# An RGCN kernel on one core: products and other uses of PSUM get three fixed banks each instead of six in one ring

## The chip, the core and the metric

The kernel runs on one core of a Trainium2 chip. The metric is the device time of one execution in microseconds (us). Of the engines, PE multiplies matrices and turns tiles (its weight loads are listed apart, as PEld), DVE works on whole tiles, ACT copies and applies functions, POOL issues the gathers, and SP issues the other transfers.

## The reference

Two layers of a relational graph convolution on 50000 nodes of 128 features, then a sum with the input and a layer norm. There are 850000 edges, sorted by their destination, each of one of 16 relations. A relation's matrix is a mixture of 8 basis matrices. Only rows below show the computation.

```python
def _rgcn_layer(h, src, dst, rel, basis, w_comp, loop_w, bias):
    W = jnp.einsum('rb,bio->rio', w_comp, basis)
    seg = dst * N_REL + rel
    agg = jax.ops.segment_sum(h[src], seg, num_segments=N_ENT * N_REL)
    agg = agg.reshape(N_ENT, N_REL, -1)
    msg = jnp.einsum('nri,rio->no', agg, W)
    return jax.nn.relu(msg + h @ loop_w + bias)

h = _rgcn_layer(x, ..., basis1, w_comp1, loop_w1, bias1)
h = _rgcn_layer(h, ..., basis2, w_comp2, loop_w2, bias2)
return _layernorm(x + h)
```

## The kernel before

The edges lie in 6250 tiles of at most 128 slots, and ten tiles (K) make a chunk, so a layer (number n, 0 or 1) has C = 625 chunks. For each tile i, POOL gathers the 128 source rows (`gather`, L254) into one of 40 places (four chunks of ten). PE multiplies them by a matrix of one-hot weights, `hot`, with 8 bases times 12 neighbouring nodes as columns: this is the tile's product (L1018), 128 x 96 in fp32, and it sums the messages by basis and node. DVE adds the product to a ring of node sums in SBUF (`add`, L950), at an offset that is read from memory. The matrix `hot` of a chunk is built on DVE (`hot_of`, L923 and L930) from the weights `pm`.

Every 512 nodes form a group, 98 in a layer, one to about 64 tiles. A group's ring columns are begun with the nodes' own loops (`lay` on ACT, L770, and `own` on DVE, L775, twice a group), copied out once all their edges are added (L792), multiplied by the basis matrices (`base`, L798) and the loop's matrix (L803), passed through relu (L810), turned back (`back`, L822) and stored (in layer 0 by ACT, L830, in layer 1 by DVE with the norm). In layer 0 alone each group's input rows are also turned (`turn`, L726, read by ACT in `turned`, L729), its loop weights combined (`combine`, L743, read by ACT, L754), and every 40 tiles the edges' weights are made (`multiply`, L668, two banks, read by ACT in `kept`, L682).

**Order.** PE, DVE, ACT and POOL run in the order in which the code emits. A loop over chunks and tiles emits the products; a tile's add is emitted twelve products later (BEHIND). All other steps are events in a heap, due at a tile's number (`planned`, `later`), and `go_on` emits what is due after each tile. A read of a bank that has been written by PE is due 12 or 18 tiles after the write.

**Banks.** PSUM has eight banks of 128 x 512 fp32. One is `fixed` (one-hot masks), one is `pn` (bases and loop). The other six are shared by all the rest through `banks`, an object of the class `Turns`. Five consecutive products (PER) share a bank, taken at the first. The taker hands over the read that is to follow (for products: all adds up to the bank's last), and the pool's rotation picks the place:

```python
def take(self, read=None):
    if len(self.held) == self.count:
        first = self.held.pop(0)
        if first is not None:
            first()
    self.held.append(read)
    return self.pool.tile([P, BANK], F32, name=self.name)
```

So a bank comes back after six takes, whoever took it, and if the read of its old content has not been emitted by then, it is emitted at once. The write then waits for that read on its engine.

Of the kernel before, what the change touches and what calls it, by code (L numbers as in the profile page):

```python
# [40 lines left out]
F32 = mybir.dt.float32  # L41
# [7 lines left out]
PSUM = bass.MemoryType.PSUM  # L49
DRAM = bass.MemoryType.DRAM  # L50

P = 128
# [3 lines left out]
K = P // WN  # L56
# [9 lines left out]
PER = 5  # L66
Q = AT // 2
BANK = 512
# [8 lines left out]
BEHIND = 12  # L77
AFTER = 18
AT_ONCE = 4
WIDE = 1  # L80
PARTS_OF = ((0, 3), (3, 5))
EPS = 1e-5
# [7 lines left out]
def tile_rgcn_resnorm(  # L90
# [20 lines left out]
    C = -(-M // (K * P))  # L111
# [106 lines left out]
                    left = less  # L218
            nc.vector.tensor_copy(split[:, n], mine)

    ps_a = ctx.enter_context(tc.tile_pool(name="ps_a", bufs=6, space=PSUM))
    ps_f = ctx.enter_context(tc.tile_pool(name="ps_f", bufs=1, space=PSUM))
    fixed = ps_f.tile([P, BANK], F32, name="fixed")
    ps_n = ctx.enter_context(tc.tile_pool(name="ps_n", bufs=1, space=PSUM))
# [2 lines left out]
    nc.vector.tensor_copy(grid, col[:, :WN])  # L227

    class Turns:
        def __init__(self, pool, name, count):  # L230
            self.pool, self.name, self.count, self.held = pool, name, count, []

        def take(self, read=None):

            if len(self.held) == self.count:
                first = self.held.pop(0)
                if first is not None:
                    first()
            self.held.append(read)
            return self.pool.tile([P, BANK], F32, name=self.name)  # L240

    class Once:
        def __init__(self, what, *args):
# [4 lines left out]
            if what is not None:  # L248
                what(*self.args)

    banks = Turns(ps_a, "pa", 6)

    def gather(to, of, idx):
        return nc.gpsimd.indirect_dma_start(  # L254
# [2 lines left out]

    def turned(h, m, sb):

        tp = ps_a.tile([P, BANK], F32, name="pa")  # L260
        nc.tensor.transpose(tp[:, :m], h, ident[:m, :m])
        hT = sb.tile([P, P], F32, name="hT")
        nc.scalar.copy(hT[:, :m], tp[:, :m])
        return hT[:, :m]
# [342 lines left out]
    def chunked():  # L607
        with (
# [20 lines left out]
            class Weights:  # L629
# [31 lines left out]

                def multiply(self):
                    m = self.m
                    self.po = [banks.take(self.keep) for _ in PARTS_OF]
                    for po, (j0, j1) in zip(self.po, PARTS_OF):
                        of = po[:, : 2 * AT * (j1 - j0) * NB].rearrange("e (n t w) -> e n t w", n=2, t=AT)
                        for j in range(j0, j1):
                            nc.tensor.matmul(  # L668
                                of[:, :, :, (j - j0) * NB : (j - j0 + 1) * NB],
                                self.is_rel[:m, j * P : (j + 1) * P],  # L670
                                each[:m],
                                start=True,
                                stop=True,
                            )
# [17 lines left out]
            class Group:  # L692
# [28 lines left out]

                def turn(self):
                    m = self.m
                    self.po = banks.take(self.keep)
                    for j in range(J):
                        nc.tensor.transpose(self.po[:, j * P : j * P + m], self.h[:m, j, :], ident[:m, :m])  # L726

# [11 lines left out]
                    )  # L739

                def combine(self):
                    self.comb = banks.take(self.combined)
                    nc.tensor.matmul(  # L743
                        self.comb[: 2 * NB, : self.cnt],
                        split[:LOOPS].rearrange("r n b -> r (n b)"),
                        self.is_rel[:LOOPS, : self.cnt],
                        start=True,
                        stop=True,
                    )
# [16 lines left out]
                    )  # L766

                def lay(self, b):
                    self.laid[b] = banks.take(self.owns[b])
                    nc.scalar.copy(self.laid[b][:, : self.cnt], self.hT[:, : self.cnt])  # L770

                def own(self, b):
# [43 lines left out]

                def back(self):
                    m = self.m
                    self.po = banks.take(self.kept)
                    by_place = self.oT[:, : self.cnt].rearrange("o (p j) -> o j p", j=J)  # L820
                    for j in range(J):
                        nc.tensor.transpose(self.po[:m, j * D : (j + 1) * D], by_place[:, j, :], ident)  # L822
# [94 lines left out]
            for n, of in enumerate((x, H1)):  # L917

                def hot_of(c):
# [15 lines left out]
                    )  # L935
                    hots[c] = hot

                def add(c, k, pa):

                    i = c * K + k  # L940
                    if i % (2 * K) == 0:
                        left = min(2, C - c) * K
                        offs = batches[c // BATCH].offs
                        nc.vector.load(at_reg[:left], offs[0:1, c % BATCH * K : c % BATCH * K + left])  # L944
                    if k == 0:
                        for one in groups:
                            assert not first(one.g) <= c <= final(one.g) or one.made
                    at = nc.vector.snap(at_reg[i % (2 * K)], min_val=0, max_val=RING - 1)
                    into = ring[:, :, ds(at, WN)]
                    nc.vector.tensor_tensor(  # L950
                        into,
                        pa[:, k % PER * NB * WN : (k % PER + 1) * NB * WN].rearrange("d (b w) -> d b w", w=WN),
                        into,
                        op=OP.add,
                    )
# [41 lines left out]
                for c in range(C):  # L997
                    if n == 0 and c:

                        next(coming, None)  # L1000
                        while ready[0] + 1 < len(ROWS) and 2 * min(C, c + FETCH + 6) > ROWS[ready[0] + 1]:
                            next(coming)
                    for to in range(0 if c == 0 else c + FETCH, min(C, c + FETCH + 1)):
                        buffer = (n * C + to) % GATHERS
                        for k in range(ks(to)):
                            gather(rows[buffer][:, k, :], of, src[:, to * K + k : to * K + k + 1])
                    g = rows[(n * C + c) % GATHERS]
                    if c == 0:
                        hot_of(0)
                        hot_of(1)  # L1010
                        if n == 0:
                            done(first_runs)
                    hot = hots.pop(c)
                    for k in range(K):
                        if k % PER == 0:
                            pa = banks.take(Once(added_up_to, c * K + k + PER - 1))
                        if k < ks(c):
                            nc.tensor.matmul(  # L1018
                                pa[:, k % PER * NB * WN : (k % PER + 1) * NB * WN],
                                g[:, k, :],  # L1020
                                hot[:, k].rearrange("e b w -> e (b w)"),
                                start=True,
                                stop=True,
                            )
                            behind.append((c * K + k + BEHIND, (c, k, pa)))
                        added_up_to(c * K + k - BEHIND)
                        if c or k == K - 1:
                            go_on(c * K + k)
                    if n == 0 and c == 3:
                        beginning.close()  # L1030
                    if n == 0 and c == C - 1:
                        done(coming)
                        count_up(pr)
                now = C * K
                while events or behind:
                    added_up_to(now - BEHIND)
                    go_on(now)
                    now += 1
                banks.held = [None] * len(banks.held)
            ordered.close()  # L1040

    def summed():
        L1 = dram.tile([N, D], F32, name="L1")
        L2 = dram.tile([N, D], F32, name="L2")
        with tc.tile_pool(name="io", bufs=2) as io, tc.tile_pool(name="sbf", bufs=2) as sb:
# [73 lines left out]
            def added(h, n, L):  # L1119


                def block(r0, p):
# [13 lines left out]
                    for e in range(ROW):  # L1136
# [3 lines left out]
                        msg = sb.tile([P, D], F32, name="msg")  # L1140
                        for b in range(NB):
                            if b % (BANK // D) == 0:
                                mb = ps_a.tile([P, BANK], F32, name="pa")
                                nc.tensor.matmul(
                                    mb[:p, :BANK],
                                    gT,
                                    BASIS[:, b : b + BANK // D, :].rearrange("p b d -> p (b d)"),
                                    start=True,
                                    stop=True,
                                )  # L1150
                            of = mb[:p, b % (BANK // D) * D : (b % (BANK // D) + 1) * D]
                            by = comp[:, e, b : b + 1]
                            if b == 0:
                                nc.vector.tensor_scalar(msg[:p], of, by, None, op0=OP.mult)
                            else:
                                nc.vector.scalar_tensor_tensor(msg[:p], of, by, msg[:p], op0=OP.mult, op1=OP.add)

                        at = tf[:p, e : e + 1]
                        tp = ps_a.tile([P, BANK], F32, name="pa")
                        nc.tensor.transpose(tp[:p, :p], at.to_broadcast([p, p]), ident[:p, :p])  # L1160
                        same = sb.tile([P, P], F32, name="same")
                        nc.vector.tensor_scalar(same[:p, :p], tp[:p, :p], at, None, op0=OP.is_equal)
# [80 lines left out]
```

## Time and profile before

| | |
|---|---|
| median of three runs | 18209.43 us (18202.78 to 18209.78) |
| the profiled execution | 18065.77 us |
| its span | 18063.9 us |
| mean granted clock of PE | 0.602 |
| busy: PE, weight loads | 8315.7 us (46%), 6301.1 us (35%) |
| busy: DVE, ACT, POOL | 6563.7 us (36%), 1621.0 us (9%), 11861.6 us (66%) |
| transfers | 1527.32 MB, 85 GB/s |

A line of the profile's groups names the line of code, the engine, the operation, what is written and read, and the count, then the busy time, the mean in ns, and the idle time of the engine just before, with what ended most of it. "issue" is idle time that ended with nothing the profile shows, "remote" one whose releaser it doesn't know. A line of the waits has the total, the count and the longest. A row of the timeline has the start, the time and in brackets the idle time before it. The starts of matmuls are recorded; their ends are modelled.

### The profile page before, as it was taken

Reading aid. Unit: us, or ns where it says so; the run is one execution under the profiler, and the core shown is the slowest. Engines: PE = TensorE matmul, PEld = TensorE weight load, DVE = VectorE, ACT = ScalarE, POOL = GpSimd, SP = SyncE. Lnnn points to the kernel's source line nnn. Section 1 sums busy time; section 2 is a strip of 40 time slices with the busy share of each in tenths; the row PEclk is TensorE's granted clock in tenths of the full one; section 3 lists DMA queues with packets and bytes.
Section 4 is the critical chain, followed back from the end, with each engine's and each line's share of the span. In section 5 each row is a group of like instructions: output and inputs, shape, how many; then the busy total and the mean of one; then the engine's idle time right before and its main releaser. Section 6 shows DMA issues by size and latency. Waiting matters only on the chain.

```text
span 18063.9 us, 132710 instructions
## 1 busy us (share of the span) xinstructions
PE 8315.7 (46%) x31484; PEld 6301.1 (35%) x31484; DVE 6563.7 (36%) x18253; ACT 1621.0 (9%) x2256; POOL 11861.6 (66%) x12540
## 2 busy tenths in 40 slices
PE   3444444444444444444444444444444444444444
PEld 2333333333333333333333333333333333333333
DVE  5444444443333333333333333333333333333333
ACT  0110011110100000010000000000000000000000
POOL 6666666666666666666666666666666666666665
PEclk7666666666666666666655555555555555555556
DMA  3333333333323322232322222222222222222222
GB/s 100 94 95 92 92 95 95 94 88 89 85 84 85 85 85 82 85 88 83 84 78 81 81 82 79 81 81 81 81 80 80 81 81 81 81 81 81 81 81 67
DMA packets 793018, 1527.32 MB, mean 85 GB/s; under 512 B 229924, under 2 KB 296342, under 8 KB 792230
## 3 DMA queue, kind: packets, MB, share of 16 engines
q0 software_dynamic: 403552, 826.82, 18.0%
q1 hardware_dynamic: 386934, 691.33, 11.6%
q8 instruction: 259, 4.24, 0.1%
q14 instruction: 529, 4.33, 0.1%
q10 hardware_dynamic: 1744, 0.60, 0.0%
HBM read 1390.97 MB, written 126.86 MB: 84 GB/s over the span
## 4 chain that ended last, share of the span: by engine, by line
issue 37%; PE 28%; another core or an unknown queue 16%; POOL 8%; DVE 5%; DMA 3%; ACT 1%; DVEq 1%; POOLq 0%; ACTq 0%; SPq 0%
PE pa L1018 18%; POOL g L254 8%; PE pn L798 8%; DVE ring L950 2%; DMA g<-H,src 2%; DVE ring L775 1%; PE pa L668 1%; PE pn L803 1%; DMA g<-in_x_dram,src 1%; ACT own L792 0%; PE pa L822 0%; DVE fixed L330 0%; DVEq L944 0%; DVE word L333 0%
## 5 line engine op out<-in xcount | busy, mean ns | idle before, releaser
L1018 PE MATMUL pa<-hot,g 128*128 128x96 f32 x25000 | 5704.8, 361 | 7613.1 <-issue 5607.3
L1018 PEld LDWEIGHTS pa<-hot,g 128*128 128x128 f32 x25000 | 5201.3, 276 | 9323.7 <-issue 7321.4
L254 POOL DMA_INDIRECT g<-in_x_dram,src x6250 | 5929.4, 949 | 3046.5 <-issue 1432.7
L254 POOL DMA_INDIRECT g<-H,src x6250 | 5895.2, 943 | 3045.9 <-issue 1428.8
L950 DVE TENSOR_TENSOR ring<-pa,ring 128x96 f32 x12500 | 3212.4, 257 | 10941.4 <-PE pa L1018 5215.2
L798 PE MATMUL pn<-own,basis 128*128 128x512 f32 x3104 | 2237.5, 799 | 508.1 <-issue 486.0
L930 DVE TENSOR_TENSOR hot<-pm,fixed 128x960 f32<-128x960 f32 x1250 | 1443.0, 1154 | 78.9 <-remote 19.2
L792 ACT COPY own<-ring 128x4096 f32<-128x4096 f32 x194 | 699.6, 3606 | 3172.0 <-DVE ring L950 2131.9
L775 DVE TENSOR_TENSOR ring<-wide,pa 128x2048 f32<-128x2048 f32 x392 | 893.7, 2280 | 84.1 <-issue 28.8
L798 PEld LDWEIGHTS pn<-own,basis 128*128 128x128 f32 x3104 | 656.1, 250 | 701.3 <-issue 696.3
L770 ACT COPY pa<-hT 128x512 f32<-128x512 f32 x392 | 230.8, 589 | 3035.4 <-DVE ring L950 1349.5
L726 PE MATMUL pa<-ident,rows 128*128 128x128 f32 x392 | 107.7, 420 | 829.6 <-ACT t L830 452.2
L810 ACT ACTIVATE oT<-pn,bias_of 128x512 f32<-128x512 f32 x196 | 134.3, 685 | 3928.0 <-PE pa L1018 2237.0
L668 PE MATMUL pa<-each,is_rel 128*128 128x128 f32 x1570 | 348.4, 377 | 291.8 <-issue 151.4
L668 PEld LDWEIGHTS pa<-each,is_rel 128*128 128x128 f32 x1570 | 300.5, 276 | 324.0 <-issue 226.2
L726 PEld LDWEIGHTS pa<-ident,rows 128*128 128x128 f32 x392 | 74.6, 223 | 845.1 <-ACT t L830 457.0
L923 DVE TENSOR_TENSOR fixed<-fixed,key 128x120 f32<-128x120 f32 x1250 | 350.4, 280 | 0.1
L822 PE MATMUL pa<-ident,oT 128*128 128x128 f32 (+1 forms) x784 | 218.6, 406 | 201.4 <-issue 133.9
L803 PE MATMUL pn<-hT,loop 128*128 128x512 f32 x392 | 263.1, 740 | 50.1 <-issue 49.9
L682 ACT COPY pm<-pa 128x192 f32<-128x192 f32 x628 | 141.0, 304 | 1063.8 <-remote 903.3
L822 PEld LDWEIGHTS pa<-ident,oT 128*128 128x128 f32 (+1 forms) x784 | 146.7, 219 | 230.2 <-issue 206.0
L597 ACT ACTIVATE sd<-mv,eps 128x4 f32<-128x4 f32 x98 | 29.1, 297 | 1929.9 <-DVE st L594 969.3
(129 smaller groups left out, 1655.8 us busy)
## 6 DMA issues: line engine op xcount, KB each, us to landing
wide<-CW SPq DMA_DIRECT2D x388, 1024.0 KB
g<-in_x_dram,src POOLq DMA_INDIRECT x6250
g<-H,src POOLq DMA_INDIRECT x6250
rows<-in_x_dram SPq DMA_DIRECT2D x194, 256.0 KB
PM<-pm SPq DMA_DIRECT2D x157, 160.0 KB
pm<-PM SPq DMA_DIRECT2D x157, 160.0 KB
H1T<-oT SPq DMA_DIRECT2D x97, 256.0 KB
H<-t SPq DMA_DIRECT2D x97, 256.0 KB
```

Of the source, the lines that this page charges most:

```text
L254: return nc.gpsimd.indirect_dma_start(out=to, out_offset=None, in_=of, in_offset=bass.IndirectOffsetOnAxis(ap=idx, axis=0))
L668: nc.tensor.matmul(of[:, :, :, (j - j0) * NB : (j - j0 + 1) * NB], self.is_rel[:m, j * P : (j + 1) * P], each[:m], start=True, stop=True,)
L770: nc.scalar.copy(self.laid[b][:, : self.cnt], self.hT[:, : self.cnt])
L775: nc.vector.tensor_tensor(ring[:, b : b + AT_ONCE, self.at : self.at + cnt], self.wide.pop(b)[:, :, :cnt], self.laid.pop(b)[:, None, :cnt] ...
L792: nc.scalar.copy(self.sums, ring[:, :, at : at + cnt])
L798: nc.tensor.matmul(self.pn[:, : self.cnt], BASIS[:, b, :], self.sums[:, b, :], start=b == 0, stop=False)
L803: nc.tensor.matmul(self.pn[:, : self.cnt], LOOP, self.hT[:, : self.cnt], start=False, stop=True)
L822: nc.tensor.transpose(self.po[:m, j * D : (j + 1) * D], by_place[:, j, :], ident)
L923: nc.vector.tensor_tensor(own[:, : ks(c)], grid[:, None, :].to_broadcast([P, ks(c), WN]), key[:, c * K : c * K + ks(c), None].to_broadcast ...
L930: nc.vector.tensor_tensor(hot[:, : ks(c)], pm[:, c % BATCH * K : c % BATCH * K + ks(c), :, None].to_broadcast([P, ks(c), NB, WN]), own[:, ...
L950: nc.vector.tensor_tensor(into, pa[:, k % PER * NB * WN : (k % PER + 1) * NB * WN].rearrange("d (b w) -> d b w", w=WN), into, op=OP.add,)
L1018: nc.tensor.matmul(pa[:, k % PER * NB * WN : (k % PER + 1) * NB * WN], g[:, k, :], hot[:, k].rearrange("e b w -> e (b w)"), start=True, st ...
```

## The change

The six places become fixed tiles, `pa0` to `pa5`. A take says among which of them it takes turns: products among the first three (`range(part[0])` with 3 in the table SECTIONS), all other uses of the two layers among the last three (OTHERS). A place that is taken again has its pending read emitted first, as before. Set-up and the unused second path take any of the six. The table's two flags (another order of a bank's products) are off, so products keep their order; the code around them is written for both.

```diff
+SECTIONS = (
+    ((3, False, False),),
+    ((3, False, False),),
+)
+OTHERS = ((3, 4, 5), (3, 4, 5))
...
-    ps_a = ctx.enter_context(tc.tile_pool(name="ps_a", bufs=6, space=PSUM))
+    ps_a = ctx.enter_context(tc.tile_pool(name="ps_a", bufs=1, space=PSUM))
...
     class Turns:
...
+        def __init__(self, tiles):
+            self.tiles, self.held, self.turn = tiles, [None] * len(tiles), {}
+
+        def take(self, read=None, among=None):
+
+            among = tuple(among or range(len(self.tiles)))
+            at = among[self.turn.get(among, 0) % len(among)]
+            self.turn[among] = self.turn.get(among, 0) + 1
+            if self.held[at] is not None:
+                self.held[at]()
+            self.held[at] = read
+            return self.tiles[at]
...
-    banks = Turns(ps_a, "pa", 6)
+    banks = Turns([ps_a.tile([P, BANK], F32, name=f"pa{i}") for i in range(6)])
...
-                    self.po = [banks.take(self.keep) for _ in PARTS_OF]
+                    self.po = [banks.take(self.keep, OTHERS[0]) for _ in PARTS_OF]
...
-                    self.po = banks.take(self.keep)
+                    self.po = banks.take(self.keep, OTHERS[self.n])
...
-                    self.comb = banks.take(self.combined)
+                    self.comb = banks.take(self.combined, OTHERS[0])
...
-                    self.laid[b] = banks.take(self.owns[b])
+                    self.laid[b] = banks.take(self.owns[b], OTHERS[self.n])
...
-                    self.po = banks.take(self.kept)
+                    self.po = banks.take(self.kept, OTHERS[self.n])
...
-                    for k in range(K):
-                        if k % PER == 0:
-                            pa = banks.take(Once(added_up_to, c * K + k + PER - 1))
+                    for at in range(K):
+                        part = SECTIONS[n][c * len(SECTIONS[n]) // C]
+                        k = at // PER * PER + (PER - 1 - at % PER if part[1] and c + 1 < C else at % PER)
+                        if at % PER == 0:
+                            pa = banks.take(
+                                Once(added_up_to, c * K + at + PER - 1), range(part[0])
+                            )
```

The lines of the new file lie 6 to 13 further down: the product is L1031, the add L959, the gather L260, the weights' multiplication L674, the turning L732, the combining L749, the base L804 and the turning back L828.

The first place is on PE in layer 0, about a quarter of the way into PE's list, where a group's weights are combined and the next weights are made. A name has the buffer's number behind it; "waits" names the engines or transfers whose semaphore the instruction waits for. Before:

```order
L743 LDWEIGHTS split_81 [waits DVE_49]
L743 MATMUL pa_22662<-is_lrel_22576,split_81 16x512 [waits Activation_49]
L1018 MATMUL pa_22649<-hot_22506,g3_96 128x96 [waits DMASW1_49]
L798 MATMUL pn_22609<-own_22492,basis_76 128x512
L1018 MATMUL pa_22649<-hot_22506,g3_96 128x96 [waits DMASW2_49]
L1018 MATMUL pa_22649<-hot_22506,g3_96 128x96 [waits DMASW3_49]
L798 MATMUL pn_22609<-own_22492,basis_76 128x512
L1018 MATMUL pa_22689<-hot_22600,g0_93 128x96 [waits DMASW4_49,DVE_49]
L668 MATMUL pa_22697<-each_80,is_rel_22580 128x16x8 [waits Activation_49]
L668 MATMUL pa_22697<-each_80,is_rel_22580 128x16x8 x2
L668 MATMUL pa_22698<-each_80,is_rel_22580 128x16x8 [waits DVE_49,PE_49]
```

The same place after:

```order
L749 LDWEIGHTS split_81
L749 MATMUL pa3_96<-is_lrel_21566,split_81 16x512
L1031 MATMUL pa2_95<-hot_21486,g3_102 128x96 [waits DMASW1_49]
L804 MATMUL pn_21583<-own_21458,basis_76 128x512
L1031 MATMUL pa2_95<-hot_21486,g3_102 128x96 [waits DMASW2_49]
L1031 MATMUL pa2_95<-hot_21486,g3_102 128x96 [waits DMASW3_49]
L804 MATMUL pn_21583<-own_21458,basis_76 128x512
L1031 MATMUL pa0_93<-hot_21574,g0_99 128x96 [waits DMASW4_49,DVE_49]
L674 MATMUL pa4_97<-each_80,is_rel_21570 128x16x8 x3
L674 MATMUL pa5_98<-each_80,is_rel_21570 128x16x8 [waits Activation_49]
```

The instructions stand in the same order. The combining no longer waits at this place, the second of the weights' banks waits for ACT where it waited for DVE and PE, and the product's new bank waits for DVE in both.

The second place is on PE in layer 1, where a group's result is turned back into a bank (`back`), between two products. Before:

```order
L1018 MATMUL pa_65248<-hot_65127,g3_96 128x96 [waits DMASW7_49,DVE_49,PE_49]
L822 MATMUL pa_65256<-ident_72,oT_65137 128x128 [waits DVE_49,PE_49,Activation_49]
L822 MATMUL pa_65256<-ident_72,oT_65137 128x128 x3
L1018 MATMUL pa_65248<-hot_65127,g3_96 128x96 [waits DMASW0_49]
L1018 MATMUL pa_65248<-hot_65127,g3_96 128x96 [waits DMASW1_49]
L1018 MATMUL pa_65248<-hot_65127,g3_96 128x96 [waits DMASW2_49]
L1018 MATMUL pa_65248<-hot_65127,g3_96 128x96 [waits DMASW3_49]
L1018 MATMUL pa_65287<-hot_65196,g0_93 128x96 [waits DMASW4_49,DVE_49,Activation_49]
```

After:

```order
L1031 MATMUL pa0_93<-hot_62268,g3_102 128x96 [waits DMASW7_49,DVE_49]
L828 MATMUL pa5_98<-ident_72,oT_62275 128x128 [waits Activation_49]
L828 MATMUL pa5_98<-ident_72,oT_62275 128x128 x3
L1031 MATMUL pa0_93<-hot_62268,g3_102 128x96 [waits DMASW0_49]
L1031 MATMUL pa0_93<-hot_62268,g3_102 128x96 [waits DMASW1_49]
L1031 MATMUL pa0_93<-hot_62268,g3_102 128x96 [waits DMASW2_49]
L1031 MATMUL pa0_93<-hot_62268,g3_102 128x96 [waits DMASW3_49]
L1031 MATMUL pa1_94<-hot_62334,g0_99 128x96 [waits DMASW4_49,DVE_49]
```

Here, too, nothing moved. The bank `pa0` follows on `pa2` and is followed by `pa1`, so a product's bank was last a product's, and the opening product waits for DVE alone, for the last add of the bank three banks ago, eleven products back.

More of the change, by code (lines that the diff above doesn't have):

```diff
@@ L229, in tile_rgcn_resnorm @@
     class Turns:
[L230 to L240, printed above, removed]
+        def __init__(self, tiles):
[8 more added lines that the diff above has]
+            return self.tiles[at]
     class Once:
@@ L258, in turned @@
     def turned(h, m, sb):
-        tp = ps_a.tile([P, BANK], F32, name="pa")
+        tp = banks.take()
         nc.tensor.transpose(tp[:, :m], h, ident[:m, :m])
@@ L936, in hot_of @@
                     hots[c] = hot
+                pair = [None]
                 def add(c, k, pa):
                     i = c * K + k
-                    if i % (2 * K) == 0:
+                    if (n, i // (2 * K)) != pair[0]:
+                        pair[0] = n, i // (2 * K)
                         left = min(2, C - c) * K
@@ L1024, in chunked @@
                             )
[L1025 to L1028, printed above, removed]
+                            if part[2] and c + 1 < C:
+                                behind.insert(len(behind) - at % PER, (c * K + at // PER * PER + PER - 1 + BEHIND, (c, k, pa)))
+                            else:
+                                behind.append((c * K + at + BEHIND, (c, k, pa)))
+                        added_up_to(c * K + at - BEHIND)
+                        if c or at == K - 1:
+                            go_on(c * K + at)
                     if n == 0 and c == 3:
@@ L1039, in chunked @@
                 banks.held = [None] * len(banks.held)
+                banks.turn.clear()
             ordered.close()
@@ L1142, in block @@
                             if b % (BANK // D) == 0:
-                                mb = ps_a.tile([P, BANK], F32, name="pa")
+                                mb = banks.take()
                                 nc.tensor.matmul(
@@ L1158, in block @@
                         at = tf[:p, e : e + 1]
-                        tp = ps_a.tile([P, BANK], F32, name="pa")
+                        tp = banks.take()
                         nc.tensor.transpose(tp[:p, :p], at.to_broadcast([p, p]), ident[:p, :p])
```

## The prediction

> **What bounds the kernel now.** I read the page's busy line and its groups first, then the list of waits, then two windows of the timeline, and last the table of windows for the two layers apart. The busy line and the four groups that each of the 12500 products passes through:
>
> ```profile
> PE 8315.7 (46%) x31484; PEld 6301.1 (35%) x31484; DVE 6563.7 (36%) x18253; ACT 1621.0 (9%) x2256; POOL 11861.6 (66%) x12540
> ...
> L1018 PE MATMUL pa<-hot,g 128*128 128x96 f32 x25000 | 5704.8, 361 | 7613.1 <-issue 5607.3
> L1018 PEld LDWEIGHTS pa<-hot,g 128*128 128x128 f32 x25000 | 5201.3, 276 | 9323.7 <-issue 7321.4
> ...
> L254 POOL DMA_INDIRECT g<-H,src x6250 | 5895.2, 943 | 3045.9 <-issue 1428.8
> L950 DVE TENSOR_TENSOR ring<-pa,ring 128x96 f32 x12500 | 3212.4, 257 | 10941.4 <-PE pa L1018 5215.2
> ```
>
> No engine is full. POOL, the fullest, waits too, and the list of waits says for whom; so does DVE's largest entry. The columns are the total, the number of waits and the longest:
>
> ```profile
> DVE ring L950 <- PE pa L1018: 5215.2, 1059, 22.6
> DVE ring L950 <- remote: 4149.8, 567, 28.9
> POOL g L254 <- remote: 1603.5, 1256, 8.9
> POOL g L254 <- PE pa L1018: 1295.0, 1639, 8.3
> ```
>
> The gather (L254) waits for a free one of its 40 tiles of rows, which a finished product frees, and the add (L950) waits for the bank's last product. Both wait for the end of products. The price without that wait is in POOL's own beat:
>
> ```profile
> 14008.18 0.94 POOL L254 DMA_INDIRECT g<-H,src  x1 [0.30 <-issue]
> 14009.42 0.94 POOL L254 DMA_INDIRECT g<-H,src  x1 [0.30 <-issue]
> ```
>
> That is 1.24 us a gather, 6250 x 1.24 = 7.75 ms a layer. What a product takes in fact comes from the table of windows, for the product line alone (busy us and records of PE, then of PEld, then the granted clock), the first row in layer 0, the second in layer 1:
>
> ```profile
> 500.00:8500.00 8000.00, 2327.39 (x11082) 2155.47 (x11083) 0.62 0.31 89
> 9500.00:17500.00 8000.00, 2754.29 (x11232) 2480.69 (x11231) 0.58 0.29 81
> ```
>
> A product is two matmul records, so a product takes 8000 / 5541 = 1.444 us in layer 0 and 8000 / 5616 = 1.425 us in layer 1: 9024 and 8903 us for 6250 products. PE's finishing of products sets the pace, 0.2 us a product above POOL.
>
> How far PE is ahead of what it has finished shows in one stretch of layer 0, first PE's weight loads, then DVE, then ACT:
>
> ```profile
> 5050.39 4.77 PEld L1018 LDWEIGHTS pa<-hot,g 128*128 128x128 f32 x22 [1.01 <-ACT pm L682]
> 5054.99 0.71 PEld L822 LDWEIGHTS pa<-ident,oT 128*128 128x128 f32 x4
> 5055.61 0.76 PEld L1018 LDWEIGHTS pa<-hot,g 128*128 128x128 f32 x6
> 5085.96 0.71 PEld L726 LDWEIGHTS pa<-ident,rows 128*128 128x128 f32 x4 [29.59 <-ACT t L830]
> ...
> 5062.94 1.79 DVE L950 TENSOR_TENSOR ring<-pa,ring 128x96 f32 x6
> 5075.52 0.26 DVE L950 TENSOR_TENSOR ring<-pa,ring 128x96 f32 x1 [10.78 <-remote]
> 5076.20 0.82 DVE L950 TENSOR_TENSOR ring<-pa,ring 128x96 f32 x3
> 5087.48 1.43 DVE L950 TENSOR_TENSOR ring<-pa,ring 128x96 f32 x5 [8.90 <-PE pa L1018]
> ...
> 5085.32 0.58 ACT L830 COPY t<-pa 128x512 f32<-128x512 f32 x1 [27.50 <-remote]
> ```
>
> PE starts nothing for 29.59 us, since the turning of the next group's rows (L726) needs a bank that ACT has not read (L830). Yet adds go on until the end of it: products already handed to PE keep coming out. So an idle stretch of PE in this trace is not lost time as such; it counts only where what PE holds runs out.
>
> **The change part by part.** The instructions on PE, DVE, ACT and POOL stay the same in number and shape, so every term is a wait.
>
> *What goes.* In layer 0 a group of 64 products takes 12.8 banks for products and 8.2 for other uses (turn, combine, two layings, back, and two for weights every 40 products). With six banks in one ring a product's bank was often last held by ACT, and the other way round. Products and others now never share a bank, and these waits go, four rows of PE's list:
>
> ```profile
> PEld pa L1018 <- ACT pm L682: 558.7, 58, 38.3
> PEld pa L726 <- ACT t L830: 457.0, 20, 33.2
> PEld pa L1018 <- ACT lrel L754: 315.2, 24, 31.9
> PEld pa L1018 <- ACT hT L729: 116.1, 13, 21.0
> ```
>
> They add up to 1447 us in 115 waits, the most that could be won. The other bound is nothing, as adds go on through them. I take the value from the two layers: layer 1 has no L668, L682, L726, L729, L743 or L754, and its products are 0.0193 us shorter, x 6250 = 120 us. If every one of these blocks cost something, all of that difference is theirs. I take **-120 us**; what hides the rest is the work that PE holds at a block's start, and it would be up to the 1447 us if that cover were not there.
>
> *What comes.* In layer 1 a group takes 12.8 banks for products and three for others. A bank came back after six takes, five or six of them products' as a rule, so that a new bank waited for add i-26 or i-21. With three banks it waits for add i-11, every time, in both layers. When DVE has added everything up to a bank's end, PE holds at most the next ten products; while DVE waits for a bank's last product, PE holds at most that bank and ten more. Behind the waiting product on PE's list stand the other products, and the base matmuls, turns and backs of the groups, for which ACT waits; POOL waits for product j-40, further back still. On DVE one thing moves: the two adds before a new take are emitted ahead of the building of one-hot weights and the layings' products, which wait for those two adds now; DVE was idle for 10941 us before adds, so I put it at nothing, and at its duration of 2 x 0.257 us per chunk, 320 us a layer, if that cover failed.
>
> What ten products are worth as cover: in series 10 x 2 x (361 + 276) ns = 12.7 us, with hidden weight loads 10 x 2 x 361 ns = 7.2 us. DVE's waits for PE of more than 10 us are the places where that runs out, 138 in layer 0 and 181 in layer 1 (sums 1875 and 2480 us). The first and last of each:
>
> ```profile
> 291.01 0.26 DVE L950 TENSOR_TENSOR ring<-pa,ring 128x96 f32 x1 [13.38 <-PE pa L1018]
> 9060.27 0.55 DVE L950 TENSOR_TENSOR ring<-pa,ring 128x96 f32 x2 [19.16 <-PE pa L1018]
> 9165.97 1.43 DVE L950 TENSOR_TENSOR ring<-pa,ring 128x96 f32 x5 [25.29 <-remote]
> 17992.48 1.14 DVE L950 TENSOR_TENSOR ring<-pa,ring 128x96 f32 x4 [15.89 <-PE pa L1018]
> ```
>
> Lower bound: nothing, if PE has enough left each time. Upper bound: at each of them PE stands still for what is over 10 us (670 us in layer 1, 1875 - 1380 = 495 in layer 0) and for the five adds that then free the bank (1.43 us, the row at 9165.97): 670 + 259 + 495 + 197 = 1621 us. I take five adds for each long wait of layer 1, 181 x 1.43 = **+259 us**, since PE holds the ten products beyond the awaited bank and loses only the way through DVE; and nothing in layer 0, where waits for ACT as long as these already stood in the same places. It is nearer to the lower end, as DVE's wait is over 12.7 us in only 101 of the 181.
>
> [...]
>
> *The sum.* -120 + 259 = +139 us. The profiled execution took 18065.8 us with a span of 18063.9; 18066 + 139 = 18205 us. The median of the runs shown, 18209.4, is 1.00795 times the profiled execution, and 18205 x 1.00795 = **18350 us**.
>
> **The rivals.** The measurement tells about 0.2%, 36 us, from no change.
>
> *Layer 0 alone gains.* The ten products are always cover enough, the new wait costs nothing, and the 120 us are won: 17946 x 1.00795 = 18088 us. For it: adds went on for 29 us with nothing started. Against it: the rows of over 20 us in which DVE got nothing at all.
>
> *The full list of PE is itself slow* (the other side, larger). Layer 1's product matmuls take 2754.29 / 11232 = 0.245 us, layer 0's 2327.39 / 11082 = 0.210 us, and layer 0 gets more done altogether:
>
> ```profile
> 500.00:4500.00 4000.00, 1770.77 (x7448) 1379.60 (x7448) 1699.94 (x4624) 412.30 (x626) 2640.23 (x2777) 0.62 0.32 93
> 4500.00:8500.00 4000.00, 1795.23 (x7464) 1389.65 (x7465) 1334.74 (x3602) 392.54 (x588) 2640.51 (x2795) 0.62 0.30 84
> 9500.00:13500.00 4000.00, 1926.41 (x6581) 1423.09 (x6580) 1386.06 (x3964) 321.68 (x396) 2647.18 (x2808) 0.58 0.29 81
> 13500.00:17500.00 4000.00, 1919.00 (x6579) 1417.69 (x6578) 1384.41 (x3960) 320.24 (x391) 2648.21 (x2808) 0.58 0.28 81
> ```
>
> 14912 matmul records in 8000 us against 13160. If that is because PE holds less there, the new rule brings it to layer 1: 8903 x (1 - 13160 / 14912) = 1046 us, still within POOL's 8903 - 7750 = 1153. With the 120 it gives 16900 x 1.00795 = 17034 us, half of it 17622. It decides once layer 1's product matmul falls clearly below 0.245 us. Against it: the clock differs too, and the kinds of matmul.
>
> *No change.* PE's pace of finishing is its own, and neither term is seen: 18209 us.
>
> *PE starves.* The upper bound, 18066 + 1621 = 19687, x 1.00795 = 19843 us. A kin of it is the clock: if layer 0's 0.62 fell to layer 1's 0.58, at 9024 us it would cost 9024 x (0.62 / 0.58 - 1) = 622 us. Against it: layer 1 has the lower clock and the shorter product. [...]
>
> **How the numbers follow.** Forecast (a loss of 0.2 to 3%): 0.36. PE starves (18750 to 19843): 0.14. No change: 0.10. Layer 0 alone gains: 0.24. The full list relieved, wholly or in part (17034 to 17950): 0.16. Slower is 0.36 + 0.14 = 0.50, same 0.10, faster 0.24 + 0.16 = 0.40. Both signs hold much, so the forecast's own range is 18250 to 18750. The range to hold 8 in 10 goes to 17450 (it leaves out the lower 0.07 of the relief) and to 18950 (it leaves out 0.11 of the starving).
>
> **What would show it.** Right: no waits of PE's products for ACT in the list; in their place rows "pa L1031 <- DVE ring L959" (the product's and the add's new lines) of some hundred us in layer 1; a product in 8000 us of layer 0 near 1.425 us, of layer 1 near 1.425 + 259 / 6250 = 1.466. Wrong: a layer 1 that gets shorter, or POOL's waits for PE nearly gone (relief), or waits for DVE of over 1000 us with the gathers' waits grown (starving).

## The result: no change

The changed kernel took 18213.39 us (median of 12 runs, 18202.67 to 18224.1), the one before 18202.78 (12 runs, 18189.99 to 18212.08): a ratio of 1.0005, interval 0.9997 to 1.0013. The forecast was 18350 us.

The waits did what the change says. The list of waits of the changed kernel (total us, number, longest us):

```profile
PEld pa L1031 <- DVE ring L959: 6152.1, 1360, 26.1
...
DVE ring L959 <- remote: 6455.6, 802, 26.2
...
DVE ring L959 <- PE pa L1031: 3064.4, 806, 19.7
...
POOL g L260 <- remote: 1619.7, 1472, 5.1
POOL g L260 <- PE pa L1031: 1503.0, 1578, 7.3
...
PEld pa L828 <- ACT pm L688: 317.8, 17, 22.3
```

The four rows of products and turns that waited for ACT, 1447 us, are gone. A part of them came back elsewhere: the turning back now waits for ACT for 318 us and the weights' multiplication for 94, where no such row of theirs had been over 4 us. PE's largest named wait is new: 6152 us for the add, 2091 of them between 500 and 8500 us (layer 0) and 3317 between 9500 and 17500 us (layer 1).

POOL's two rows, 3123 us, are nearly the old 2899. DVE's waits before its adds are nearly the old ones too: 6455.6 us for a releaser that the profile doesn't know and 3064.4 for PE's products, 9520 together, where 4149.8 and 5215.2 made 9365. More than 10 us at once (whatever the releaser) DVE waits 167 times in layer 0 and 178 times in layer 1, against 138 and 181 before. The line of the adds among the groups, then the first and last of these waits in each layer:

```profile
L959 DVE TENSOR_TENSOR ring<-pa,ring 128x96 f32 x12500 | 3215.6, 257 | 11072.2 <-remote 6455.6
```

```profile
260.61 0.26 DVE L959 TENSOR_TENSOR ring<-pa,ring 128x96 f32 x1 [12.70 <-remote]
9139.74 1.43 DVE L959 TENSOR_TENSOR ring<-pa,ring 128x96 f32 x5 [17.10 <-PE pa L1031]
9224.54 0.26 DVE L959 TENSOR_TENSOR ring<-pa,ring 128x96 f32 x1 [14.03 <-PE pa L1031]
18160.11 0.26 DVE L959 TENSOR_TENSOR ring<-pa,ring 128x96 f32 x1 [16.87 <-remote]
```

Some 4700 us more in PE's named waits made no difference to the time. They aren't 4700 us more of standing still, either: the waits of the same line without a name (issue) fell from 7321 to 3747 us, so that PE's idle time before the loads of products grew by 1076 us, from 9323.7 to 10399.5:

```profile
L1031 PEld LDWEIGHTS pa<-hot,g 128*128 128x128 f32 x25000 | 5198.5, 290 | 10399.5 <-DVE ring L959 6152.1 <-issue 3746.5 <-DVE ring L781 164.3
```

The table of windows for the product line, first layer 0, then layer 1:

```profile
500.00:8500.00 8000.00, 2466.09 (x10985) 2255.47 (x10985) 0.60 0.29 88
9500.00:17500.00 8000.00, 2538.50 (x11144) 2338.21 (x11144) 0.58 0.26 80
```

That is 1.457 and 1.436 us a product, 0.9% and 0.8% more than in the trace of before. The two profiled executions as wholes differ by as much (18217.6 to 18063.9 us of span), while the medians agree. So this difference is one between two executions and not the change's; between the layers it leaves 0.1%, 8 us, where -120 in one and +259 in the other were forecast.

### The profile page after: what moved, and what is told of

It reads as the page before. It is cut to its first block, busy times and chain, and to the rows that moved or that the text cites. A ratio compares the mean times of both kernels' runs of the same rounds, so it can differ in the third digit from the quotient of the medians.

```text
span 18217.6 us, 130879 instructions
## 1 busy us (share of the span) xinstructions
PE 8259.5 (45%) x31484; PEld 6305.2 (35%) x31484; DVE 6620.1 (36%) x18253; ACT 1601.6 (9%) x2256; POOL 11853.8 (65%) x12540
## 3 DMA queue, kind: packets, MB, share of 16 engines
q0 software_dynamic: 403552, 826.82, 16.0%
## 4 chain that ended last, share of the span: by engine, by line
another core or an unknown queue 38%; issue 22%; PE 20%; DVE 15%; DVEq 2%; POOL 2%; DMA 1%; ACT 1%; ACTq 0%; SPq 0%; POOLq 0%
PE pa L1031 12%; DVE ring L959 8%; PE pn L804 6%; DVE ring L781 2%; DVEq L953 2%; POOL g L260 2%; PE pa L674 1%; ACT own L798 1%; DVE fixed L929 1%; DVE fixed L336 1%; PE pn L809 1%; DVE word L339 1%; DMA g<-in_x_dram,src 0%; DVE st L600 0%
## 5 line engine op out<-in xcount | busy, mean ns | idle before, releaser
L1031 PE MATMUL pa<-hot,g 128*128 128x96 f32 x25000 | 5670.4, 383 | 8652.2 <-DVE ring L959 5606.2
L1031 PEld LDWEIGHTS pa<-hot,g 128*128 128x128 f32 x25000 | 5198.5, 290 | 10399.5 <-DVE ring L959 6152.1
L260 POOL DMA_INDIRECT g<-in_x_dram,src x6250 | 5921.7, 947 | 3148.7 <-issue 1316.0
L260 POOL DMA_INDIRECT g<-H,src x6250 | 5895.2, 943 | 3116.5 <-issue 1293.3
L959 DVE TENSOR_TENSOR ring<-pa,ring 128x96 f32 x12500 | 3215.6, 257 | 11072.2 <-remote 6455.6
L804 PE MATMUL pn<-own,basis 128*128 128x512 f32 x3104 | 2270.1, 815 | 329.9 <-issue 327.1
L804 PEld LDWEIGHTS pn<-own,basis 128*128 128x128 f32 x3104 | 665.4, 257 | 483.2 <-issue 482.5
L674 PE MATMUL pa<-each,is_rel 128*128 128x128 f32 x1570 | 361.8, 390 | 302.3 <-issue 180.8
L674 PEld LDWEIGHTS pa<-each,is_rel 128*128 128x128 f32 x1570 | 315.3, 290 | 328.6 <-issue 217.6
L828 PE MATMUL pa<-ident,oT 128*128 128x128 f32 (+1 forms) x784 | 207.7, 420 | 358.6 <-ACT pm L688 314.3
L828 PEld LDWEIGHTS pa<-ident,oT 128*128 128x128 f32 (+1 forms) x784 | 166.7, 240 | 363.2 <-ACT pm L688 317.8
L836 ACT COPY t<-pa 128x512 f32<-128x512 f32 x98 | 58.0, 591 | 1692.0 <-remote 992.5
L760 ACT COPY lrel<-pa 16x512 f32<-16x512 f32 x98 | 56.1, 572 | 1702.9 <-PE pa L1031 828.4
```

The costliest lines, as they stand in the source:

```text
L260: return nc.gpsimd.indirect_dma_start(out=to, out_offset=None, in_=of, in_offset=bass.IndirectOffsetOnAxis(ap=idx, axis=0))
L674: nc.tensor.matmul(of[:, :, :, (j - j0) * NB : (j - j0 + 1) * NB], self.is_rel[:m, j * P : (j + 1) * P], each[:m], start=True, stop=True,)
L804: nc.tensor.matmul(self.pn[:, : self.cnt], BASIS[:, b, :], self.sums[:, b, :], start=b == 0, stop=False)
L959: nc.vector.tensor_tensor(into, pa[:, k % PER * NB * WN : (k % PER + 1) * NB * WN].rearrange("d (b w) -> d b w", w=WN), into, op=OP.add,)
L1031: nc.tensor.matmul(pa[:, k % PER * NB * WN : (k % PER + 1) * NB * WN], g[:, k, :], hot[:, k].rearrange("e b w -> e (b w)"), start=True, st ...
```

## The experiments

The kernel before took 15.80 to 15.82 ms on three of the chips and 18.06 to 18.22 ms on the others, with the same program. Each ratio below is against the kernel before on the same chip, and each experiment names which kind it was.

**The kernel before once more** (no edit).

> The kernel before, unchanged, profiled a second time. Its first profiled execution took 18065.8 us against a median of 18202.8. If that was a stray, this one should lie within 36 us of the median, and the product's time by windows should be about 1.436 us in layer 1 instead of 1.425; if profiling itself makes this kernel 0.8% faster, it should be near 18066 again.

15823.27 us against 15824.11, on a chip of the quicker kind; the profiled execution took 15805.42. So profiling doesn't make this kernel 0.8% faster on this chip, and something larger came to light. On this chip PE waits for the gathers and POOL hardly waits beyond its usual gap:

```profile
PEld pa L1018 <- DMA g<-H,src: 3669.0, 4058, 5.1
PEld pa L1018 <- DMA g<-in_x_dram,src: 2910.3, 3141, 5.3
...
POOL g L254 <- issue: 2409.9, 7911, 0.3
```

No wait of that last row, the largest of POOL's rows, is over 0.3 us, the usual gap between two gathers. 12500 x 1.249 us is 15.6 ms: here the gathers' issue is the pace.

**One layer at a time.** The table gives the layer without the split one ring of six fixed places (here layer 1, and layer 0 in the second run):

```diff
-    ((3, False, False),),
+    ((6, False, False),),
...
-OTHERS = ((3, 4, 5), (3, 4, 5))
+OTHERS = ((3, 4, 5), (0, 1, 2, 3, 4, 5))
```

> Three and three banks in layer 0, one ring of six fixed places in layer 1. Theory A (PE finishes products at a pace of its own, and neither the waits for ACT nor the smaller lead is felt): within 0.2% of before. Theory B (two effects that cancel, as forecast but of equal size): about 120 us or 0.7% faster, all of it in layer 0.

> One ring of six fixed places in layer 0, three and three banks in layer 1. Theory A: within 0.2% of before. Theory B: 120 to 260 us or 0.7 to 1.4% slower, all of it in layer 1.

1.0006 (0.9996 to 1.0015) and 1.000 (0.999 to 1.001), on the same chip of the quicker kind. There are no two effects that cancel there.

**Two banks for products, four for the rest.**

```diff
-    ((3, False, False),),
-    ((3, False, False),),
+    ((2, False, False),),
+    ((2, False, False),),
...
-OTHERS = ((3, 4, 5), (3, 4, 5))
+OTHERS = ((2, 3, 4, 5), (2, 3, 4, 5))
```

> Two banks for products and four for the rest, in both layers: a new bank waits for add i-6, so PE holds five products beyond the awaited bank instead of ten. Theory A: under 1% slower, since five products at 1.43 us are 7 us and the way through DVE takes 1.4 to 2 us. Theory B, and every theory in which PE's lead covers DVE's waits: with five products less, all of DVE's waits over 5 us count, about 400 in each layer with 1700 to 2000 us beyond the 5 us, so 10 to 20% slower.

> Two banks for products and four for the rest once more, for a chip at 18.2 ms if this is one: theory A within 1% there; theory B 10 to 20% slower. At 15.8 ms it should repeat the 0.16%.

> Two banks for products and four for the rest. At 15.8 ms 0.15% slower, twice. At 18.2 ms: theory A (the lead is not felt) within 0.5%; theory B (the lead covers what comes late) over 3% slower, since DVE waits for PE there for up to 29 us and PE holds five products less.

1.0016 (1.0006 to 1.0026) and 1.0015 (1.0005 to 1.0024) on two quicker chips, 1.0008 (0.9998 to 1.0017) on one at 18.06 ms, whose list of waits has:

```profile
PEld pa L1031 <- DVE ring L959: 9412.7, 1686, 26.3
PE pa L1031 <- DVE ring L959: 8780.3, 1621, 26.1
DVE ring L959 <- remote: 8271.7, 1112, 24.4
```

PE's loads wait for the add for half of the span, and the kernel is 0.17% slower at most; the 0.15% on the quicker chips are small, but beyond the noise. The lead of products covers next to nothing at 18 ms. The theory of a lead, which asked for over 3%, falls.

**Half of the gathers.** Only even tiles are gathered, and an odd tile is multiplied with its neighbour's rows, which leaves out half of the gathered data; for before and for the changed kernel.

```diff
-                        for k in range(ks(to)):
+                        for k in range(0, ks(to), 2):
...
-                                g[:, k, :],
+                                g[:, k - k % 2, :],
```

> The kernel before with every second gather left out (an odd tile is multiplied with its neighbour's rows), so POOL has half its work and is not the pace on any chip. On a chip where the kernel before takes 15.8 ms, theory C (there the gathers' issue at 1.249 us sets the pace, 12500 x 1.249 = 15.6 ms) expects it clearly faster, 10 to 14 ms, by what PE or DVE then allow; where it takes 18.2 ms, theory C expects no change within 1%, since PE's finishing sets the pace there and POOL waits for it.

> The changed kernel with every second gather left out, to be held against the same of before: with the gathers gone as a bound, the banks could matter. Theory A (PE has a pace of its own; waits for ACT and the lead are not felt): within 0.5% of the one of before. Theory B (ten products are too small a cover): 2 to 10% slower than it. A third theory, that the change was worth something but was hidden behind the gathers: 1 to 5% faster than it.

0.547 (0.5461 to 0.5479) and 0.5555 (0.5546 to 0.5564) on one chip at 15.80 ms. First, the same 12500 products, adds and banks take 8.65 ms, less than the 10 to 14 expected. Secondly, with the gathers out of the way the change does cost: 8779.0 / 8645.4 = 1.0155, between the 0.5% and the 2% that the theories gave. The gathers of layer 0 read `in_x_dram`, those of layer 1 `H`. Their rows have the least, median and longest duration in ns, then the starts of the first and the last; the ring of six, then three and three:

```profile
L254 POOL DMA_INDIRECT g<-in_x_dram,src x3125: 938/945/1612, 47.5 to 4477.8; - x196
L254 POOL DMA_INDIRECT g<-H,src x3125: 938/945/995, 4506.1 to 8588.1; - x196
```

```profile
L260 POOL DMA_INDIRECT g<-in_x_dram,src x3125: 938/945/1653, 47.4 to 4595.3; - x196
L260 POOL DMA_INDIRECT g<-H,src x3125: 938/945/1009, 4631.7 to 8724.7; - x196
```

Layer 1 begins 126 us later, and the whole span is 132 us longer (8643.4 to 8775.2). So the loss is in layer 0, which is the other way round than the forecast had it. And a chip of the slower kind:

> The kernel before with every second gather left out, as the other's yardstick on the same chip: 0.547 of before on a chip at 15.8 ms. On a chip at 18.2 ms, if PE's finishing sets the pace there, 0.98 to 1.0 of before; if the gathers take part in it, well below.

0.535 (0.5341 to 0.5359) at 18.22 ms. There, too, the gathers take half of the time with them. The forecast's bound, PE's own finishing, would have left it as it was. The granted clock was higher in these runs, 0.75 and 0.73 in place of 0.62 and 0.60, but the clock isn't what halves the time: with doubled products (below) it was 0.70 and nothing was gained, with one base in place of eight it was 0.525 and nothing was lost.

**Which banks cost, with half of the gathers.** Four and two, and two and four (the table as above, with other numbers).

> The changed kernel with every second gather left out, and four banks for products and two for the rest. With three and three that was 0.5555 of before, and the ring of six 0.547. If the loss comes from the lead of ten products (a wait for add i-11), a wait for add i-16 takes most of it back: 0.547 to 0.550. If it comes from the other uses having fewer banks, two banks are worse than three: over 0.557.

> The changed kernel with every second gather left out, and two banks for products and four for the rest. If the loss of three and three (0.5555 of before against 0.547) comes from the other uses having too few banks, four give it back: 0.547 to 0.552 in spite of a lead of only five products. If it comes from the lead, two banks are worst: over 0.565. If both count, it lies near 0.556 or above, with the loss now in waits of products for the add.

> The changed kernel with every second gather left out. At 15.8 ms it repeats 0.5555 of before. On a chip at 18.2 ms, where the ring of six gave 0.535 and two banks with four for the rest 0.539: 0.540 to 0.545 if the number of banks for the other uses decides, 0.535 to 0.538 if the products' lead does.

Four for products and two for the rest: 0.5586 (0.5577 to 0.5596) on another chip at 15.81 ms, the worst. Two and four, on the same chip as the ring of six at 18.22 ms: 0.539 against 0.535, 9825.69 / 9751.55 = 1.0076. Three and three, at 18.06 ms: 0.5335 (0.5326 to 0.5343), below both of the ranges expected. It can't be compared to half a per cent with the chip at 18.22, so whether three and three cost anything on the slower kind stays open; nothing like 1.55% shows. At 15.8 ms, then, the lead alone isn't the cause: four banks lengthen it, and the kernel loses more. With two banks for the other uses the turn waits for the layings' product, which it doesn't with three. The waits of PE with three and three, then with four and two, at 15.8 ms:

```profile
PEld pa L1031 <- DVE ring L959: 2569.4, 1234, 13.9
```

```profile
PEld pa L1031 <- DVE ring L959: 2145.4, 1217, 14.7
...
PEld pa L732 <- DVE ring L781: 311.3, 57, 19.0
PEld pa L732 <- issue: 129.4, 34, 9.7
```

The wait for the add falls by 424 us and the turn's takes its place. How the 1.55% of three and three divides between the lead and the other uses isn't settled, since two and four was run on the other kind of chip only.

**PE's work.** Every product's matmul twice, in both kernels, and seven of eight base matmuls left out of before.

```diff
-                            nc.tensor.matmul(
+                            for _ in range(2):
+                                nc.tensor.matmul(
```

```diff
-                    for b in range(NB):
+                    for b in range(1):
                         later(end + AFTER + 2 * b, self.base, b)
```

> The kernel before with every product's matmul done twice into the same place (the second writes over the first), so PE's own work per product doubles and nothing else changes. Meant to make PE the pace on a chip where the gathers are it. There a recorded pair of weight load and matmul comes every 0.35 us when PE runs freely, so four pairs make 1.4 us a product and the time 17 to 20 ms. If it stays at 15.8 ms, PE has more to spare than its records show.

> The changed kernel with every product's matmul done twice, to be held against the same of before. Theory A (with PE's own work the pace, a lead of ten products, now 40 pairs, is cover enough): within 0.3% of it. Theory B (what PE loses at a bank's opening is lost for good when PE is the pace): 1 to 4% slower.

> The kernel before with every product's matmul done twice into the same place. At 15.8 ms it was no slower. At 18.2 ms: if PE's own work sets the pace there, as the forecast had it, 30% slower or more (two more pairs of 0.35 us on 1.43 us are half as much again); if the pace is set by what each product waits for and reports, which is the same here, within 2%.

> The kernel before with seven of the eight base matmuls of each group left out (2744 of 3136 matmuls of 128x512, which leaves out that part of the result). At 799 ns each that is 2.2 ms of PE's recorded time. If PE's own work is the pace (a chip at 18.2 ms): 1.3 to 2.2 ms faster. If the gathers are the pace (a chip at 15.8 ms): within 0.5% of before.

At 15.8 ms: 1.0001 (0.9991 to 1.0011) and 1.0006 (0.9997 to 1.0016) with every product twice, and 0.9988 (0.9979 to 0.9998) with one base in place of eight. For the first, 17 to 20 ms had been expected. The timeline with doubled products shows the room between two gathers:

```profile
13003.14 0.94 POOL L254 DMA_INDIRECT g<-H,src  x1 [0.30 <-issue]
13003.19 0.69 PE L1019 MATMUL pa<-hot,g 128*128 128x96 f32 x4 [0.49 <-DMA g<-H,src]
13003.71 1.05 PE L798 MATMUL pn<-own,basis 128*128 128x512 f32 x2
13004.39 0.94 POOL L254 DMA_INDIRECT g<-H,src  x1 [0.30 <-issue]
```

Four product matmuls and two of a base are started between one gather's issue and the next, 1.25 us later, and PE waits for the gather before them. So this pair was no test of the banks with PE as the pace; PE never became it. At 18.06 ms the doubled products made 1.0122 (1.0106 to 1.0139), for 25000 more matmuls:

```profile
L1019 PE MATMUL pa<-hot,g 128*128 128x96 f32 x50000 | 9649.8, 343 | 5424.9 <-issue 4963.9
```

220 us for work that is recorded with 9649.8 - 5704.8 = 3945 us more on this line, against the 30% that PE's pace would have meant. PE's work isn't the bound there either.

**What the slower pace goes with.** All gathers, but PE reads (and waits for) every second one only; and places for three chunks of rows instead of four.

```diff
-                                g[:, k, :],
+                                g[:, k - k % 2, :],
```

```diff
-GATHERS = 4
+GATHERS = 3
```

> The kernel before with all gathers issued, but odd tiles multiplied with their neighbour's rows, so that PE waits for every second gather only (half of the gathered rows are not used). At 15.8 ms, where the gathers' issue is the pace, no change within 0.3%. At 18.1 to 18.2 ms: if each gather costs 1.43 us there by itself, within 1% of before; if PE's wait for each gather is what costs, down to the gathers' issue, 15.7 to 16.2 ms.

> The kernel before with places for three chunks of gathered rows instead of four, thirty tiles. At 15.8 ms, where a product starts 2.5 us after its gather, no change within 0.3%. At 18.1 to 18.2 ms: no change within 0.5% if the pace is a rate that the gathers set; 10 to 30% slower if it is the delay of 57 us from a gather's issue to its place's release.

0.9974 (0.9964 to 0.9984) at 18.06 ms: but for 0.3%, PE's waits for gathers aren't it. 0.9997 (0.9987 to 1.0006) at 18.21 ms: it is a rate and no loop of delays, which with 30 places in place of 40 would have been slower. What is left is the number of gathers that are issued, or the data that they bring: halving the gathers also took the gathers' queue from 826.82 to 416.82 MB, and no run parts the two. With all of them, and half of them read, POOL still stops behind PE, although half of its gathers write to places that no product reads:

```profile
POOL g L254 <- remote: 1816.2, 846, 8.7
POOL g L254 <- PE pa L1018: 660.9, 474, 7.9
```

Why a gather takes 1.43 us there and 1.25 us elsewhere, and why PE's reports come late with it, these runs don't show. That stays open.

## Why the prediction was wrong

*What bounds the kernel.* This is the step that failed, and the two terms with it. "PE's finishing of products sets the pace" took the wait that ends last, POOL's for PE, for PE's work. The rows were right, the step from a wait to a cause was not: halving the gathers took 46% off the time where PE's finishing "set the pace", doubling PE's matmuls added 1.2%. A hint lay in the trace, in the stretch with nothing started for 29.59 us. PE's last matmul before it is modelled to end at 5056.54 us, yet adds still came 19 to 22 us later; that was read as cover for a busy PE, not as a sign that the ends of products keep another time than PE's work. The adds did not go on to the end of the stretch, either. This is the last one, and the 8.90 us in the forecast's row at 5087.48 are DVE's wait after it:

```profile
5078.33 0.25 DVE L950 TENSOR_TENSOR ring<-pa,ring 128x96 f32 x1
```

*The gain of 120 us* (forecast in layer 0). Sized from the difference of two layers, on the assumption that blocks of PE must cost something. Measured at 15.8 ms: 1.0006 with layer 0 alone changed. At 18.2 ms the two layers moved alike within 0.1%. So the 1447 us of waits were worth nothing. The cover that was named, work that PE holds, needn't have been enough for that: in the stretch above it ended before the wait did. PE's time isn't on the path.

*The loss of 259 us* (forecast in layer 1). The new wait came as described, with the add, in the rows that were named, but with 3317 us in 8000 us of layer 1 in place of some hundred, and in layer 0 as well. DVE's long waits stayed: 178 over 10 us in layer 1 and 167 in layer 0. But each cost nothing in place of 1.43 us. Two banks, with half the lead, cost nothing beyond the noise at 18.06 ms either. The lower end of the term, nothing, was the right one, for another reason than the one given: not that PE has work enough left, but that the time it stands still isn't on the path.

*The clock* (the kin of "PE starves"). A fall in layer 0 from 0.62 to 0.58 was put at 622 us. By the windows it was 0.60 there after the change, and 0.58 in layer 1 as before, and layer 0's product grew by only 0.1%, 8 us in 8000, more than layer 1's. The mean granted clock went from 0.602 to 0.597 at 18 ms, and was 0.616 and 0.618 at 15.8 ms in the kernel before and with layer 0 or layer 1 changed.

*The rivals.* "No change", with a chance of 0.10, is what happened. Of its reason, that the pace is PE's own and that neither term enters it, the second half was right and the first wasn't. "Layer 0 alone gains" is out, since by the windows layer 0 gained no more than layer 1. The full list of PE was no brake: with each bank of products held to add i-11, the product's matmul in layer 1 fell from 0.245 us to 2538.50 / 11144 = 0.228, while in layer 0 it rose from 0.210 to 0.224, and no time was won. The first sign of "PE starves" came, waits for the add of over 1000 us, and it starved nobody: POOL's waits for PE hardly grew.

*The offset of 1.00795* between the profiled execution and the median was carried into the number. The changed kernel's profiled execution, 18219.45 us, lies on its median, and that of the kernel before on the quicker chip within 0.12% of its median. The kernel before took 18058.7, 18062.8 and 18211.3 us (medians) on one chip at three times, each steady in itself. So its pace also moves by 0.8% from one time to another, the size of the offset. That the first trace and the first times stand on either side of such a move is likely, and not shown.

## What to carry to other kernels

Before pricing waits on an engine, find out by the smallest possible change whether its work is the pace: half of the suspected operations, or twice as many. A wait that "ends last" names who reports late, not what made it late; here POOL waited for PE, and without half of the gathers that POOL itself issues the same products were finished in about half of the time. And a change that trades one kind of wait for another on an engine off the path is worth nothing, however many milliseconds the list of waits shows; here 6152 us of a new wait came, and the ratio was 1.0005. That holds while the engine is off the path: with half of the gathers gone, at 15.8 ms, the same change cost 1.55%.

## What the runs showed of the hardware

The same program takes 15.80 to 15.82 ms on some chips and 18.06 to 18.22 ms on others, at granted clocks of 0.616 and 0.60. The difference in time is 14 to 15%, that in the clock 2 to 3%. On the quicker ones PE stands waiting for gathers, 6579 us in the two rows shown above; on the slower ones it hardly does, 272 us in the two rows of the first trace:

```profile
PEld pa L1018 <- DMA g<-H,src: 185.5, 153, 3.2
...
PEld pa L1018 <- DMA g<-in_x_dram,src: 86.8, 82, 3.8
```

There the ends of products come late instead: DVE waits for more than 10 us before an add 319 times in the first trace, for PE's products for up to 22.6 us; on the quicker chip its longest wait for them is 11.1 us, with 7992.6 us in 2125 waits. On a quicker chip PE has room for twice the product matmuls, 25000 more, within the same 15.81 ms.
